# Another emission plan for a four-layer graph attention kernel: up to six weights per group, preparation begun in one-head steps, a tighter plan for late steps, another order of the last steps

## Chip, core and metric

The kernel runs on one core of one Trainium2 chip. The metric is device time in microseconds (us) of one execution; the median of several runs is given.

The engines are called by the names of the profile: PE is TensorE, DVE is VectorE, ACT is ScalarE, POOL is GpSimd, SP is SyncE, which here only issues transfers. Each engine works through its own instructions in the order in which the program issued them; engines wait for each other by semaphores.

## What is computed

Sixteen inputs x[b] of 1024 nodes with 256 features pass through four graph attention layers that share one adjacency matrix. All is fp32. Layers 0 and 2 have four heads of 64 features, layers 1 and 3 one head of 256. In short:

```python
for l in range(4):                                   # heads H = 4, 1, 4, 1
    h = relu(layernorm(x))                           # over the 256 features
    q = h @ W[l]                                     # split into H heads
    e = leaky_relu(q @ a_src [rows] + q @ a_dst [columns])
    attn = softmax(where(adj, e, -inf), over columns)
    x = x + elu(attn @ q)                            # layer 3: relu in place of elu
```

Layers 0 and 1 mask with adj > 0, layers 2 and 3 with adj != 0.

## The kernel before

**Steps.** A step is one layer of one input, so there are 16 x 4 = 64 steps, numbered 0 to 63 in the order of `order_of_steps`. Four inputs are in flight at a time (four streams); a stream's next layer can be prepared only when its last step has been added into x. The order takes turns over the streams, so that four-head steps and one-head steps mostly alternate. Steps 0, 1, 2 have four heads; in places two four-head steps meet (13 and 14, 21 and 22, 29 and 30, ...). The last ten steps before the change have 4, 1, 4, 1, 1, 4, 1, 4, 1, 1 heads.

**Weights.** The exponential of a leaky sum is written as a maximum of two products. With a row factor `g` (one value per target node, the same on all partitions), a column factor `rcol` (one value per source node) and the mask, a weight tile of 128 source nodes by 1024 target nodes is one DVE instruction:

```python
nc.vector.scalar_tensor_tensor(w, g, rcol[:, jc, h:h+1], mask[:, jc, :], op0=ALU.max, op1=ALU.mult)   # L250
```

A head has eight such tiles, so a four-head step has 32 and a one-head step 8. They lie in a ring of `WBUFS` = 19 buffers. `g` is in PSUM (two buffers): it is written to DRAM as `grow` (L227), fetched back to all partitions as `gs` (L239, two buffers) and copied to PSUM by ACT (L245, `broadcast`).

**Aggregation.** Every step has eight groups (`aggregate`). In a four-head step a group is one half of the target nodes of one head: four blocks of 128 nodes, each over eight weight tiles. In a one-head step it is one block of 128 nodes over all eight tiles. The matmuls (L266) write `acc` (two PSUM buffers), and ACT evicts it into `y` (L270). The ratio of `y` to its last column is the attention output. Below, "32 AGG2.4" means step 32, head 2, the group that starts at block 4.

**Preparation of a step** (`preparation`), in 18 pieces: statistics of x (DVE L161 `bn_stats`, L162 `bn_aggr`, then four POOL instructions, L165 to L169, that give `rstd` and `shift`), `normalise` in two halves (ACT L175, four instructions each, into a tile of a ring of three that `finish` shares), transposes (PE L183, with relu into `hT` by ACT L184), projections of eight blocks (PE L195, evicted into `whx` and `sd` by ACT L197 to L204, multiplied by POOL L206), `factors` (rcol, gcol) and `rows` (transposed gcol, written to `grow`).

**End of a step** (`finish`), in seven pieces that are issued during the next step: the reciprocal (DVE L287), the scaling of y and the negative part (POOL L291, L296), its exponential (ACT L300), and the sum into x (DVE L306 and POOL L307; in layer 3 DVE L309 and the store of the result by SP, L310, and the load of the stream's next input).

**The order of the work** is written out by a planner. Before every group it takes care that the weights of the group's head have been issued; after it, it issues what is due in `finish`, then what is due in the preparation of later steps (`prepare`, from a sorted `agenda`), and then some weights ahead: four in a four-head step, two in a one-head step, as far as buffers are free by program order (`done["free"] + WBUFS`). The due times are counted in groups: piece k of step n + 2 is due `PREPARATION[k]` groups after the begin of step n, or after its middle where the stream's last step is step n - 1 or n. A head's `g` can be issued once the whole preparation of its step has been. `fetch_heads` issues the `gs` transfers up to two heads ahead of `g`; it is called after `rows` and after every `g`.

## Time and profile before

| | us |
|---|---|
| median of 3 runs | 2754.75 (2754.04 to 2758.51) |
| profiled execution | 2758.29 |
| its span | 2756.5 |
| PE busy, weight loads busy | 2581.3, 2268.5 |
| DVE, ACT, POOL busy | 1984.5, 1199.6, 896.6 |
| weights (L250, DVE, 1280 tiles), busy | 1543.3 |
| `bn_stats`, `bn_aggr` (DVE, 512 each), busy | 200.7, 92.8 |
| aggregation matmuls, projections, transposes (PE), busy | 1965.4, 515.8, 155.4 |

A busy time is the time in which at least one instruction of the group ran. An engine's idle time is put down to the engine whose work released it last. Idle time of an engine costs nothing while another one sets the pace, so a view of the whole says less than one of a stretch: the first 95 us prepare the masks and the weights of the layers, the rest are the 64 steps of about 40 us each.

### The profile page before, as it was taken

The page shows a single profiled execution, that of the slowest core. Times are in us where ns is not written, and L with a number is a line of the kernel's source. Part 1 is how long each engine was busy: PE and PEld are TensorE (multiplying, and loading weights), DVE is VectorE, ACT ScalarE, POOL GpSimd, SP SyncE. Part 2 cuts the span into 40 slices and gives each one's busy share as a digit, 9 for nine tenths or more (in the row PEclk, how much of TensorE's full clock was granted, in tenths as well). Part 3 has the DMA queues.
Part 4 walks back from the last instruction along what each step waited for, and adds up shares of the span by engine and source line. Part 5 has one row for each costly group of instructions (what it writes and reads, how often), then busy time and mean ns, then how long its engine had stood idle before and what let it go on. Part 6 is the DMA issues. An engine that isn't in the chain of part 4 may idle for free.

```text
span 2756.5 us, 88771 instructions
## 1 busy us (share of the span) xinstructions
PE 2581.3 (94%) x40080; PEld 2268.5 (82%) x40080; DVE 1984.5 (72%) x2569; ACT 1199.6 (44%) x3265; POOL 896.6 (33%) x909
## 2 busy tenths in 40 slices
PE   1789988999999999999999999999999999999997
PEld 1688777888888888888888888888888888888876
DVE  5596855767966779747977679767797488775772
ACT  0534444444444444544444445444444444444341
POOL 0223333343332343342242343333323333433221
PEclk9999999999999999999999999999999999999998
DMA  4111010012211210111211111002112111101101
GB/s 138 62 49 40 10 40 25 25 36 67 72 36 44 71 49 25 41 39 47 88 41 48 62 40 41 33 17 71 56 49 71 34 46 64 34 17 39 56 25 39
DMA packets 63674, 130.08 MB, mean 47 GB/s; under 512 B 6208, under 2 KB 41792, under 8 KB 63296
## 3 DMA queue, kind: packets, MB, share of 16 engines
q1 hardware_dynamic: 60608, 123.35, 13.4%
q8 instruction: 315, 5.16, 0.8%
q10 hardware_dynamic: 2688, 1.05, 0.2%
q14 instruction: 63, 0.52, 0.1%
HBM read 106.95 MB, written 17.43 MB: 45 GB/s over the span
## 4 chain that ended last, share of the span: by engine, by line
PE 72%; DVE 14%; DMA 6%; ACT 4%; issue 3%; POOL 1%; DVEq 0%; ACTq 0%; SPq 0%; POOLq 0%
PE acc L266 53%; PE pp L195 15%; DVE w L250 11%; DMA gs<-grow 4%; PE pp L183 3%; DMA grow<-gT 2%; DVE bn L161 1%; ACT t L300 1%; ACT g L245 1%; DVE t L306 1%; DVE mv L162 1%; ACT whx L197 1%; DMA a_bc<-in_L_gnn_a 1%; ACT whx L201 0%; ACT y L270 0%
## 5 line engine op out<-in xcount | busy, mean ns | idle before, releaser
L266 PE MATMUL acc<-whx,w 128*64 128x65 f32 x36864 | 1965.4, 242 | 77.9 <-DVE w L250 56.9
L266 PEld LDWEIGHTS acc<-whx,w 128*64 128x64 f32 x36864 | 1764.3, 145 | 265.5 <-DVE w L250 78.7
L250 DVE SCALAR_TENSOR_TENSOR w<-g,rcol,mask 128x1024 f32<-128x1024 f32 x1280 | 1543.3, 1273 | 523.4 <-ACT g L245 432.7
L270 ACT ACTIVATE y<-acc 128x260 f32<-128x260 f32 (+1 forms) x512 | 196.8, 384 | 1071.1 <-PE acc L266 1069.8
L195 PE MATMUL pp<-wx,hT 128*128 128x258 f32 (+1 forms) x2048 | 515.8, 395 | 2.9 <-ACT hT L184 2.7
L291 POOL TENSOR_TENSOR y<-y,r 128x1024 f32<-128x1024 f32 x128 | 243.0, 1899 | 716.1 <-DVE r L287 716.1
L195 PEld LDWEIGHTS pp<-wx,hT 128*128 128x128 f32 x2048 | 378.3, 192 | 78.1 <-ACT hT L184 15.7
L307 POOL TENSOR_TENSOR x<-x,t 128x1024 f32<-128x1024 f32 x96 | 226.8, 2362 | 408.2 <-DVE t L306 399.6
L206 POOL TENSOR_TENSOR whx<-whx 128x256 f32<-128x256 f32 x256 | 157.5, 618 | 471.2 <-ACT whx L204 471.2
L175 ACT ACTIVATE t<-x,shift,rstd 128x256 f32<-128x256 f32 x512 | 264.8, 588 | 78.7 <-POOL x L307 56.6
L245 ACT ACTIVATE g<-gs 128x1024 f32<-128x1024 f32 x160 | 163.5, 1022 | 129.5 <-DMA gs<-grow 128.0
L197 ACT ACTIVATE whx<-pp,nbias 128x4 f32<-128x4 f32 (+1 forms) x512 | 135.5, 265 | 181.3 <-PE pp L195 169.7
L161 DVE BATCH_NORM_STATS2 bn<-x 128x6 f32<-128x256 f32 x512 | 200.7, 392 | 2.4 <-DMA x<-in_x 2.4
L183 PE MATMUL pp<-ident,t 128*128 128x128 f32 x1024 | 155.4, 284 | 34.0 <-ACT t L175 18.9
L183 PEld LDWEIGHTS pp<-ident,t 128*128 128x128 f32 x1024 | 111.3, 141 | 78.8 <-ACT whx L201 28.0
L184 ACT ACTIVATE hT<-pp 128x512 f32<-128x512 f32 x256 | 145.5, 593 | 19.2 <-PE pp L183 18.8
L306 DVE SCALAR_TENSOR_TENSOR t<-t,y 128x1024 f32<-128x1024 f32 x96 | 118.4, 1233 | 35.4 <-ACT t L300 35.3
L287 DVE RECIPROCAL r<-y 128x32 f32<-128x32 f32 (+1 forms) x64 | 17.6, 276 | 160.0 <-ACT y L270 159.9
L201 ACT ACTIVATE whx<-pp,whx 128x256 f32<-128x256 f32 x256 | 121.7, 475 | 0.0
L166 POOL TENSOR_TENSOR rstd<-rstd,neghalf 128x8 f32<-128x8 f32 x64 | 106.7, 1668 | 5.3
L162 DVE BATCH_NORM_AGGREGATE mv<-bn 128x2 f32<-128x6 f32 x512 | 92.8, 181 | 16.9
L296 POOL TENSOR_SCALAR t<-y 128x1024 f32<-128x1024 f32 x96 | 101.7, 1060 | 8.5
(37 smaller groups left out, 533.0 us busy)
## 6 DMA issues: line engine op xcount, KB each, us to landing
gs<-grow SPq DMA_DIRECT2D x160, 512.0 KB
x<-in_x SPq DMA_DIRECT2D x16, 1024.0 KB
out<-x SPq DMA_DIRECT2D x32, 512.0 KB
a_raw<-in_adj SPq DMA_DIRECT2D x8, 512.0 KB
a_bc<-in_L_gnn_a ACTq DMA_DIRECT2D x8, 128.0 KB
wx<-in_L_gnn_W SPq DMA_DIRECT2D x4, 256.0 KB
grow<-gT SPq DMA_DIRECT2D x32, 16.0 KB
grow<-gT SPq DMA_DIRECT2D x32, 4.0 KB
```

The source lines that it names most:

```text
L161: nc.vector.bn_stats(st["bn"][:, c, :], xs[b][:, c, :])
L175: nc.scalar.activation(xn[:, q, :], xs[b][:, c, :], AF.Identity, bias=st["shift"][:, c:c + 1], scale=st["rstd"][:, c:c + 1])
L183: nc.tensor.transpose(pt[:, q, :], st["xn", half][:, q, k * P:(k + 1) * P], ident)
L195: nc.tensor.matmul(pw, lhsT=st["hT", half][:, k, q * P:(q + 1) * P], rhs=wx[l][:, k, :], start=(k == 0), stop=(k == K - 1))
L197: nc.scalar.activation(whx[:, c, :, D], pw[:, F + H:F + 2 * H], AF.Exp, bias=nbias[l], scale=slope)
L206: nc.gpsimd.tensor_tensor(whx[:, c, :, 0:D], whx[:, c, :, 0:D], whx[:, c, :, D:D + 1].to_broadcast([P, H, D]), op=ALU.mult)
L245: nc.scalar.activation(g, state[n]["gs", h], AF.Copy)
L250: nc.vector.scalar_tensor_tensor(w, state[n]["g", h], state[n]["rcol"][:, jc, h:h + 1], masks[LAYERS[steps[n][1]][3]][:, jc, :], op0=ALU.m ...
L266: nc.tensor.matmul(acc[o % P:o % P + cols, q, :], lhsT=st["w", h, jc][:, o:o + cols], rhs=st["whx"][:, jc, h, :], start=(jc == 0), stop=(j ...
L270: nc.scalar.activation(st["y"][:, i0:i0 + per, h, :], acc, AF.Copy)
L291: nc.gpsimd.tensor_tensor(yh, yh, r[:, :, None].to_broadcast([P, HALF * H, D]), op=ALU.mult)
L307: nc.gpsimd.tensor_add(xh, xh, e)
```

## The change

- `bn_aggr` goes: mean and variance of the two halves that `bn_stats` gives are combined by POOL, in ten instructions of 8 columns in place of four.
- `normalise` gets a ring of two tiles for itself, `finish` another one of two, in place of a common ring of three; `WBUFS` becomes 18.
- Every step gets a time of begin: 8 (n - 2) groups, three groups earlier if step n - 3 has one head, later if the stream's last step demands it (five groups after that step's end, eight for a new input). Preparation is planned from it, by `PREPARATION`, or by the tighter `LATE` where the begin was put off. By this, steps 3, 5, 6, 8, 54, 56 and 63 are late ones.
- The `gs` transfers of a step may start right after `rows`; its first `g` comes two groups later, when the preparation is declared done by an empty last piece.
- Up to six weights ahead per group in four-head steps, three in one-head steps.
- The store of a result and the next load become pieces of their own, due in group 4.
- The last ten steps have another order of streams; the numbers of heads in them are 1, 4, 1, 4, 4, 1, 4, 1, 1, 1.

The diff:

```diff
--- before.py
+++ after.py
@@ -36,8 +36,10 @@
 SHIFT = 60.0
 EXP_SHIFT = math.exp(SHIFT)
 STREAMS = 4
-WBUFS = 19
-PREPARATION = (0, 0, 1, 2, 3, 3, 4, 4, 5, 5, 5, 5, 6, 6, 7, 7, 8, 9)
+WBUFS = 18
+
+PREPARATION = (0, 0, 2, 3, 4, 4, 5, 5, 6, 6, 6, 6, 7, 7, 8, 8, 9, 10, 10, 12)
+LATE = (0, 0, 1, 1, 2, 2, 3, 3, 3, 3, 3, 3, 4, 4, 4, 4, 5, 6, 6, 8)
 
 
 LAYERS = [
@@ -155,21 +157,29 @@
 
         def stats(half):
             if half == 0:
-                st["mv"] = small.tile([P, C, 2], F32, name="mv")
                 st["bn"] = small.tile([P, C, 6], F32, name="bn")
+            bn = st["bn"]
             for c in range(half * HALF, (half + 1) * HALF):
-                nc.vector.bn_stats(st["bn"][:, c, :], xs[b][:, c, :])
-                nc.vector.bn_aggr(st["mv"][:, c, :], st["bn"][:, c, :])
+                nc.vector.bn_stats(bn[:, c, :], xs[b][:, c, :])
             if half == 1:
+
+                m0, s0, m1, s1 = (bn[:, :, i] for i in (1, 2, 4, 5))
                 rstd = st["rstd"] = small.tile([P, C], F32, name="rstd")
-                nc.gpsimd.tensor_scalar(rstd, st["mv"][:, :, 1], EPS, None, op0=ALU.add)
+                shift = st["shift"] = small.tile([P, C], F32, name="shift")
+                dev = small.tile([P, C], F32, name="dev")
+                nc.gpsimd.tensor_tensor(dev, m0, m1, op=ALU.subtract)
+                nc.gpsimd.tensor_tensor(dev, dev, dev, op=ALU.mult)
+                nc.gpsimd.tensor_scalar(dev, dev, 0.25, EPS, op0=ALU.mult, op1=ALU.add)
+                nc.gpsimd.tensor_tensor(rstd, s0, s1, op=ALU.add)
+                nc.gpsimd.tensor_scalar(rstd, rstd, 1.0 / F, None, op0=ALU.mult)
+                nc.gpsimd.tensor_tensor(rstd, rstd, dev, op=ALU.add)
                 nc.gpsimd.tensor_tensor(rstd, rstd, neghalf, op=ALU.pow)
-                shift = st["shift"] = small.tile([P, C], F32, name="shift")
-                nc.gpsimd.tensor_tensor(shift, st["mv"][:, :, 0], rstd, op=ALU.mult)
-                nc.gpsimd.tensor_scalar(shift, shift, -1.0, None, op0=ALU.mult)
+                nc.gpsimd.tensor_tensor(shift, m0, m1, op=ALU.add)
+                nc.gpsimd.tensor_tensor(shift, shift, rstd, op=ALU.mult)
+                nc.gpsimd.tensor_scalar(shift, shift, -0.5, None, op0=ALU.mult)
 
         def normalise(half):
-            xn = st["xn", half] = prep.tile([P, HALF, F], F32, name="t4", bufs=3)
+            xn = st["xn", half] = prep.tile([P, HALF, F], F32, name="xn")
             for q in range(HALF):
                 c = half * HALF + q
                 nc.scalar.activation(xn[:, q, :], xs[b][:, c, :], AF.Identity,
@@ -231,7 +241,10 @@
             out += [lambda half=half, k=k: transpose(half, k) for k in range(K)]
             out += [lambda c=c: project(c) for c in range(half * HALF, (half + 1) * HALF)]
 
-        return list(zip(PREPARATION, out + [factors, rows], strict=True))
+
+        out += [factors, rows, lambda: fetch_heads(n + 1), lambda: None]
+        at = LATE if begin[n] > 8 * (n - 2) else PREPARATION
+        return [(begin[n] + k, piece) for k, piece in zip(at, out, strict=True)]
 
     def fetch(n, h):
 
@@ -292,7 +305,7 @@
                                     op=ALU.mult)
             if l < L - 1:
 
-                e = st["e", half] = prep.tile([P, HALF * H, D], F32, name="t4", bufs=3)
+                e = st["e", half] = prep.tile([P, HALF * H, D], F32, name="e")
                 nc.gpsimd.tensor_scalar(e, yh, 0.0, -3.0e38, op0=ALU.min, op1=ALU.max)
 
         def exponential(half):
@@ -307,6 +320,8 @@
                 nc.gpsimd.tensor_add(xh, xh, e)
                 return
             nc.vector.scalar_tensor_tensor(xh, yh, 0.0, xh, op0=ALU.max, op1=ALU.add)
+
+        def store(half):
             nc.sync.dma_start(
                 out=out[b, half * HALF * P:(half + 1) * HALF * P, :].rearrange(
                     "(c p) f -> p c f", p=P), in_=xs[b][:, half * HALF:(half + 1) * HALF, :])
@@ -315,7 +330,8 @@
 
         return [(0, divide), (0, lambda: scaled(0)), (1, lambda: scaled(1)),
                 (1, lambda: exponential(0)), (2, lambda: exponential(1)),
-                (2, lambda: add(0)), (3, lambda: add(1))]
+                (2, lambda: add(0)), (3, lambda: add(1))] + (
+                    [(4, lambda: store(0)), (4, lambda: store(1))] if l == L - 1 else [])
 
 
 
@@ -328,28 +344,28 @@
     tiles = [(n, h, jc) for n, (b, l) in enumerate(steps) for h in range(LAYERS[l][0])
              for jc in range(C)]
     place = {t: i for i, t in enumerate(tiles)}
-    done = {"tiles": 0, "g": 0, "gs": 0, "free": 0, "prepared": 0, "wanted": 0}
+    done = {"tiles": 0, "g": 0, "gs": 0, "rows": 0, "free": 0, "prepared": 0}
     agenda = []
 
     def prepare(upto):
 
-        while agenda and (agenda[0][0] <= upto or agenda[0][1] < done["wanted"]):
+        while agenda and agenda[0][0] <= upto:
             _, n, piece, last = agenda.pop(0)
             piece()
             if last:
                 done["prepared"] = n + 1
-                fetch_heads()
-
-    def plan(n, at):
+
+    def plan(n):
         new = preparation(n)
-        agenda.extend((at + k, n, piece, i == len(new) - 1) for i, (k, piece) in enumerate(new))
+        agenda.extend((at, n, piece, i == len(new) - 1) for i, (at, piece) in enumerate(new))
         agenda.sort(key=lambda a: a[:2])
 
-    def fetch_heads():
-
+    def fetch_heads(below=0):
+
+        done["rows"] = max(done["rows"], below)
         while done["gs"] < min(done["g"] + 2 * C, len(tiles)):
             n, h, _ = tiles[done["gs"]]
-            if n >= done["prepared"]:
+            if n >= done["rows"]:
                 break
             fetch(n, h)
             done["gs"] += C
@@ -363,8 +379,7 @@
                 if n >= done["prepared"]:
                     if i < done["g"] or not must:
                         break
-                    done["wanted"] = n + 1
-                    prepare(-1)
+                    prepare(max(a[0] for a in agenda if a[1] == n))
                 broadcast(n, h)
                 done["g"] += C
                 fetch_heads()
@@ -375,21 +390,27 @@
 
     for b in range(STREAMS):
         load(b)
-    ready_at = [-1] * len(steps)
-    last = {}
+    last, begin = {}, []
     for n, (b, l) in enumerate(steps):
-        ready_at[n] = last.get(b % STREAMS, -9)
+
+        early = n > 2 and LAYERS[steps[n - 3][1]][0] == 1
+        begin.append(8 * (n - 2) - (3 if early else 0) if n > 1 else -99)
+        if b % STREAMS in last:
+
+            begin[n] = max(begin[n], 8 * (last[b % STREAMS] + 1) + (8 if l == 0 else 5))
+        if n > 2:
+            begin[n] = max(begin[n], begin[n - 1] + (5 if begin[n] > 8 * (n - 2) else 3))
         last[b % STREAMS] = n
-    for n in range(2):
-        plan(n, -99)
-        prepare(0)
     ending = []
     with tc.manual_schedule():
+        for planned in (1, 2):
+            plan(planned - 1)
+            prepare(-1)
         for n in range(len(steps)):
             for k, (h, i0, per) in enumerate(groups(n)):
-
-                if n + 2 < len(steps) and k == (0 if ready_at[n + 2] < n - 1 else 4):
-                    plan(n + 2, 8 * n + k)
+                while planned < len(steps) and begin[planned] <= 8 * n + k:
+                    plan(planned)
+                    planned += 1
                 emit_tiles(place[n, h, C - 1] + 1, must=True)
                 aggregate(n, h, i0, per)
                 if i0 + per == C:
@@ -397,7 +418,7 @@
                 while ending and ending[0][0] <= k:
                     ending.pop(0)[1]()
                 prepare(8 * n + k)
-                ahead = 4 if per > 1 else 2
+                ahead = 6 if per > 1 else 3
                 emit_tiles(min(done["tiles"] + ahead, done["free"] + WBUFS))
             for _, piece in ending:
                 piece()
@@ -408,16 +429,11 @@
 
 def order_of_steps(B, L):
 
+
     depth = B // STREAMS * L
     one = [[(k // L * STREAMS + s, k % L) for k in range(depth)] for s in range(STREAMS)]
-    at = [0] * STREAMS
-    turns = [0, 1, 2, 0, 3, 2] + [0, 1, 2, 3] * depth
-    steps = []
-    for s in turns:
-        if at[s] < depth:
-            steps.append(one[s][at[s]])
-            at[s] += 1
-    return steps
+    turns = [0, 1, 2, 0, 3, 2] + [0, 1, 2, 3] * (depth - 4) + [1, 0, 3, 2, 1, 0, 3, 2, 1, 3]
+    return [one[s].pop(0) for s in turns]
 
 
 _OUT = ((16, 1024, 256), "float32")
```

## The prediction

> **What bounds the kernel now.** I read the page first (busy shares and slices), then the busy time by windows, then the matrix engine's own waits in three stretches, then VectorE's timeline around one pair of steps.
>
> ```profile
> PE 2581.3 (94%) x40080; PEld 2268.5 (82%) x40080; DVE 1984.5 (72%) x2569; ACT 1199.6 (44%) x3265; POOL 896.6 (33%) x909
> ...
> PE   1789988999999999999999999999999999999997
> ...
> DVE  5596855767966779747977679767797488775772
> ...
> PEclk9999999999999999999999999999999999999998
> ```
>
> PE is busy 94% of the span, so a change of order can win back only its idle 175 us. The dips are in the first ten slices and the last one.
>
> ```profile
> 0.00:95.00 95.00, 31.59 (x152) 24.28 (x153) 42.84 (x105) 19.27 (x59) 14.34 (x32) 0.98 0.38 120
> 95.00:300.00 205.00, 181.81 (x3652) 161.71 (x3651) 172.54 (x199) 80.84 (x211) 61.57 (x64) 0.96 0.13 42
> 300.00:530.00 230.00, 207.47 (x3322) 180.01 (x3322) 150.82 (x193) 98.55 (x268) 72.32 (x67) 0.96 0.09 27
> ```
>
> Window length, then PE busy first. The start to 95 us (63 us idle) is not touched. From 95 to 530 PE idles 23.2 + 22.5 = 45.7 us at a clock of 0.96. PE's waits by releaser (us, times, longest), for 95 to 530, then 530 to 2330, then 2330 to the end:
>
> ```profile
> PE acc L266 <- DVE w L250: 35.8, 49, 0.9
> PE pp L183 <- ACT t L175: 3.1, 4, 2.7
> ```
> ```profile
> PE acc L266 <- DVE w L250: 13.1, 20, 0.9
> PE acc L266 <- ACT y L270: 12.1, 14, 1.2
> ```
> ```profile
> PE acc L266 <- DVE w L250: 7.9, 15, 1.2
> PE acc L266 <- ACT y L270: 4.4, 4, 1.6
> ```
>
> So early PE waits for weights. In the middle it loses 36 us in 1800, a third of it to ScalarE, which stands in front of an eviction while it waits for a fetch. VectorE has room on average; it is late in places:
>
> ```profile
> 354.57 1.23 DVE L306 SCALAR_TENSOR_TENSOR t<-t,y 128x1024 f32<-128x1024 f32 x1 [4.62 <-ACT t L300]
> 378.10 9.63 DVE L250 SCALAR_TENSOR_TENSOR w<-g,rcol,mask 128x1024 f32<-128x1024 f32 x8 [22.30 <-ACT g L245]
> ```
>
> Here it idles 22.3 us in a one-head step and then falls behind in the four-head step after it.
>
> **The Trainium skill.** "TensorE: Matmul & The Clock Gate" (specification table at its head) gives ScalarE, VectorE and GpSimd a strict first-in-first-out queue; the trace agrees: ScalarE idled 128.0 us in front of `g` copies for the `gs` transfer. The same page, Part 1, says idleness lowers PE's clock; the 0.96 of the early windows against 1.00 later agrees. "SBUF — State Buffer" (SBUF: two separate sides) says a VectorE instruction with two SBUF inputs locks out a GpSimd one that reads SBUF. `w` has one tensor input in PSUM, so the new small GpSimd operations should not slow it; only L306 could meet them. No run here shows that.
>
> **The change, part by part.** Prices: `w` 1543.3/1280 = 1.206 us; `bn_stats` 0.392; a pair with `bn_aggr` 4.25 us for eight; L306 1.23; PE group of a four-head step 3.8 us, of a one-head step 3.6 (rows of the timeline); preparation on PE 10.1 us (four double projections of 1.94, two transpose pairs of 1.03, one of 0.27); `t` (L175) 2.1 us per half; `g` 1.0.
>
> *Statistics.* 512 `bn_aggr` go. VectorE gets 4.25 - 8 x 0.392 = 1.1 us per preparation, 70 us in all, worth something only where VectorE is late. GpSimd gets ten operations for four: six at 0.205, three at 0.25, `pow` 1.67, that is 3.65 against 2.37 us, and with gaps 0.09 a piece 4.5 against 2.7. The chain to `shift` is 1.8 us longer at the GpSimd end and 1.1 shorter at the VectorE end: at the start +1 us. Later, `normalise` stands two groups (about 10 us) after `stats`, which hides it. In a late step (LATE: one group) it does not: there ScalarE stands at L175, and PE's transposes behind it wait some 3.5 us, as the 2.7 above already shows. Behind a standing L175 on ScalarE are the eviction of the last group and the next `g`; PE has two `acc` slots, so it notices after one group. The ten operations read strided columns of `bn`, which no row shows; at 0.2 to 0.3 us each (the 128x8 rows) the chain is 4 to 5 us. GpSimd rises from 33% to 36%; its other work has 67% idle time as cover.
>
> *Steps 0 to 2* (four heads each). VectorE needs 96 x 1.206 = 116 us and PE 92 + 28 = 120 from 104 us on, so both must run without bubbles. Four weights per group let a bubble in at each `g` (1.4, 3.4, 1.8, 5.9 us before 251). With six, `g` of the next head is issued a group earlier. By queue order VectorE then runs through: from 97.6, 32 tiles and 3.1 us of statistics end at 139; step 1's at 180; step 2's at 228. PE ends step 2 near 237; the trace has 251. Gain 14.
>
> *Steps 3 to 8.* `rows` comes two groups before the first `g`, so ScalarE no longer stands for the transfer (grow and gs, 6 us). The first weights of step 6 come about 12.7 us before its group 0, against 4.8 now (378.1 to 382.9). Against that stand new waits: transposes of steps 5, 6, 8 behind late statistics, 3.5 + 1 + 3.4, and weights late by 2 to 3 us at the ends of steps 4 and 6. Summed by queue order, step 9 begins some 25 us earlier than now, 11 of them here. I take 22 for both, 10 to 32, since clock recovery is included.
>
> *Steps 9 to 53.* Fourteen four-head steps that follow a one-head step now get their first `g` after group 4 instead of group 1. VectorE, counted from the end of group 4: first `w` 3.3 (transposes 1.0, two hT 1.2, `g` 1.0), head 0 complete at 16.1 with statistics of 3.1 between; PE wants it after one transpose pair, three groups, three double projections and another pair (1.0 + 3 x 3.6 + 1.9 + 2.9 + 1.9 = 18.6). Between heads PE has two groups and two pieces of preparation, 7.6 + 3 to 4 us, VectorE eight tiles, 9.6, and every second head two L306. So head 1 is ready at 25.9 and wanted at 29.4; `g2` stands behind a `normalise`, ready 29.3, so head 2 at 38.9, wanted 42.2; head 3 at 51.0, wanted 53.7; the next step's eight tiles at 60.6, wanted 61.6. All hold, by 1 to 4 us. Where two four-head steps meet (21/22, 37/38) the second then waits about 7 us, by the same count that gives 2.9 for now; after an early begin (13/14, 29/30, 45/46) 2.3 against 6.2. Over both kinds nothing changes. What goes is the ScalarE wait: 12.1 to about 2. Gain 10 (0 to 18).
>
> *One buffer for weights less, own buffers for `xn` and `e`.* 18 still hold two heads and two tiles; the last tiles of a head wait a group longer where VectorE is far ahead anyway, costing nothing while the margins above hold. The split ends L175's waits for x<-x,t (56.6 us, 15 times); they lie beside PE work, and I count them within the 10.
>
> *Stores* are issued one or two groups later, so SP's queue with the `gs` fetches no longer stands behind them. The next x load follows 5 us later; its statistics come four groups (about 20 us) after, and its transfer took 6.1 us in the chain of waits. Zero; without that cover up to 5 us for each of 12 loads.
>
> *Last steps.* Now 18 us of waits from 2330 on. Step 63's owner finishes layer 2 as step 60 instead of 61, and three one-head steps end the run, so weights for 61 and 62 are early; step 63's last tile is late by about 1 instead of some 6. New: late statistics before 54 and 56, 3.5 each, and one four-head meeting, 57/58, 5. About 13 remain: gain 5, with the clock 6 (-4 to 12).
>
> Sum: 1 - 22 - 10 - 6 = -37. The profiled execution took 2758.3 (span 2756.5 and 1.8 around it), so 2721; the median of the runs is 3.5 lower, so **2718**.
>
> **Rivals.** *A, half of it:* the bubbles of steps 0 to 2 go, but elsewhere each removed fetch wait returns as a wait on `shift` or on the projections' PSUM slots. For it: L175 already waited 21.6 us for `shift`. Against it: only three waits. -14: 2741. *B, weights start too late:* the slack of 2.7 us in the four-head steps is my count of ScalarE's queue. If `g` comes one one-head group (5.0 us) later, each of the 20 steps so treated loses 2.3: 46, less the 37 gained, +9: 2764; two groups later, 7.3 each, 2860. It decides from about 4.6 us of delay. For it: VectorE's 22.3 us gap shows what a late `g` does, and one-head steps now start VectorE 7 us later than the trace. Against it: the fetch is done by then. *C, it doesn't do what it says:* where buffers bind, groups emit two tiles, not six, and only the statistics saving is left, hidden by PE: within 5 us. Against it: at heads' ends six fit.
>
> **How the numbers follow.** A measurement of this kernel can tell about 0.2%, 5.5 us. Forecast 0.53 (own range 2703 to 2735), A 0.22, C 0.08, B 0.17. The forecast and A are faster: 0.75; same 0.08; slower 0.17. The range runs from full early and middle gains, 2699, to B a little over its one-group case, 2768.
>
> **What would show it.** Right: PE waits on `w` before 530 fall from 35.8 to about 22; waits on y (L270 before) in the middle from 12.1 to 2; step 9 starts near 500 instead of 525; `t` waits on `shift` grow. Wrong: PE waits on `w` between 530 and 2330 well above 13.1, at the four-head steps after a one-head step (B); or `pp` waits on ACT `xn` above 20 us (A).

## Result: slower, and the profile after

The changed kernel takes 2781.65 us (median of 4 runs, 2777.85 to 2785.33), the kernel before on the same chip 2754.39. The ratio is 1.0098, with an interval of 1.0079 to 1.0117. Slower by 27 us, where 37 us of gain were forecast. The profiled execution of after took 2777.85 (span 2776.1), so it is 19.6 us longer than the profiled one before: the profile shows a little less of the loss than the medians do.

The page of after, busy shares and slices, as for before:

```profile
PE 2577.5 (93%) x40080; PEld 2274.2 (82%) x40080; DVE 1918.1 (69%) x2057; ACT 1211.5 (44%) x3265; POOL 985.7 (36%) x1293
...
PE   1699999999999998999999999999999999999998
...
PEclk9899999999999999999999999999999999999999
```

PE does the same work, VectorE 66 us less, GpSimd 89 us more. PE's dips to 8 in the third, sixth and seventh slices are gone, and a new one stands in the sixteenth; the clock is lower in the second slice, where the steps begin. So the change did what it says, and the loss is not spread evenly. To place it I read from the timeline the end of the first eviction of all (ACT L270 in before, L283 in after), of the first one of step 9, and of the last ones of steps 53 and 63 (us):

| stage | before | after | difference | forecast |
|---|---|---|---|---|
| start to the first eviction | 112.3 | 127.9 | +15.6 | +1 |
| to the first eviction of step 9 (called steps 0 to 8) | 424.2 | 387.3 | -36.9 | -22 |
| to the last eviction of step 53 (steps 9 to 53) | 1806.9 | 1852.0 | +45.1 | -10 |
| to the last eviction of step 63 | 402.4 | 398.1 | -4.3 | -6 |

Two stages gained, one of them more than forecast. Two lost, and each loss has its place in the trace.

**The start.** VectorE's first weights, before and then after (timeline, start and length in us, in brackets the idle time ahead and what ended it):

```profile
97.59 9.62 DVE L250 SCALAR_TENSOR_TENSOR w<-g,rcol,mask 128x1024 f32<-128x1024 f32 x8 [26.89 <-ACT g L245]
```
```profile
112.53 3.67 DVE L263 SCALAR_TENSOR_TENSOR w<-g,rcol,mask 128x1024 f32<-128x1024 f32 x3 [42.89 <-ACT g L258]
```

`g` comes 15 us later. In before, the preparations of steps 0 and 1 are issued ahead of `with tc.manual_schedule()`, and ScalarE's instructions do not stand in the order in which the program is written: the first copy of `g` comes ahead of the evictions of step 1's last projections (ScalarE's timeline):

```profile
96.50 1.05 ACT L245 ACTIVATE g<-gs 128x1024 f32<-128x1024 f32 x1
...
98.88 0.30 ACT L197 ACTIVATE whx<-pp,nbias 128x4 f32<-128x4 f32 x1
```

In after they are issued inside that block, where the written order holds. ScalarE has the preparation of step 0 done at 88.7 and then goes on with step 1:

```profile
88.72 0.27 ACT L235 ACTIVATE gT<-pp 32x128 f32<-32x128 f32 x1 [1.02 <-PE pp L233]
92.52 4.04 ACT L185 ACTIVATE xn<-x,shift,rstd 128x256 f32<-128x256 f32 x8 [3.54 <-POOL shift L179]
96.46 1.05 ACT L194 ACTIVATE hT<-pp 128x512 f32<-128x512 f32 x2
...
111.32 0.27 ACT L235 ACTIVATE gT<-pp 32x128 f32<-32x128 f32 x1 [1.02 <-PE pp L233]
111.49 1.95 ACT L258 ACTIVATE g<-gs 128x1024 f32<-128x1024 f32 x2
```

The first copies of `g` stand behind the whole of that, up to step 1's own `gT`.

**The middle.** PE's waits in after between 530 and 2330 us (us, times, longest), as for before:

```profile
PE acc L279 <- DVE w L263: 29.9, 39, 0.9
PE pp L233 <- POOL gcol L228: 22.2, 10, 3.0
PE pp L193 <- ACT whx L214: 5.2, 22, 0.2
PE pp L193 <- ACT whx L211: 4.7, 22, 0.2
PE pp L205 <- ACT gT L235: 3.7, 7, 0.6
PE pp L193 <- ACT xn L185: 2.7, 2, 2.6
```

The wait for ScalarE's `y`, 12.1 in before, is gone, as forecast. In its place PE stands 22.2 us for `gcol`, a line that before does not have in this stretch, and 16.8 us more for `w`. The `gcol` stops are seven of 2.95 us (in preparations during steps 15, 20, 23, 31, 36, 39, 47) and three of 0.5. GpSimd's timeline shows one of them, with PE's row below:

```profile
1422.47 0.21 POOL L170 TENSOR_TENSOR dev<-bn 128x8 f32<-128x8 f32 x1
...
1424.20 1.67 POOL L176 TENSOR_TENSOR rstd<-rstd,neghalf 128x8 f32<-128x8 f32 x1
...
1426.12 1.23 POOL L178 TENSOR_TENSOR shift<-shift,rstd 128x8 f32<-128x8 f32 x1
1427.44 0.24 POOL L179 TENSOR_SCALAR shift<-shift 128x8 f32<-128x8 f32 x1
1427.64 1.90 POOL L304 TENSOR_TENSOR y<-y,r 128x1024 f32<-128x1024 f32 x1
1429.63 1.04 POOL L309 TENSOR_SCALAR e<-y 128x1024 f32<-128x1024 f32 x1
1430.75 0.29 POOL L228 TENSOR_SCALAR gcol<-gcol 128x32 f32<-128x32 f32 x1
```
```profile
1431.09 0.40 PE L233 MATMUL pp<-ident,gcol 128*32 128x128 f32 x1 [2.95 <-POOL gcol L228]
```

From 1422.47 GpSimd runs with no gap over 0.1 us: the ten operations of another step's statistics, then the second half's scaling of `finish` (L304, L309), and only then the 0.29 us of `gcol`. ScalarE had delivered `gcol` at 1426.45. A GpSimd of which 36% is busy is late here because of what stands ahead in its queue. Over all preparations of the stage the trace shows the same: in the seven stops of 2.95 us the other step's statistics and the scaling both stand in one unbroken run ahead of `gcol`, in the three of 0.5 us the statistics alone, and everywhere else neither, and PE does not stop. By the plan the seven are the places where this step and the one after it both begin without the three groups' lead, so that the next step's statistics come one group ahead of this one's `factors`.

The clock adds to it. Busy time by windows around the same stop (window length, PE busy first; PEclk is the column ahead of the last two):

```profile
1427.00:1430.60 3.60, 1.14 (x6) 0.65 (x4) 0.29 (x1) 0.38 (x1) 3.42 (x4) 1.00 0.00 0
1430.60:1434.00 3.40, 2.91 (x8) 2.35 (x9) 2.21 (x1) 3.18 (x6) 2.68 (x3) 0.51 0.02 7
1434.00:1444.00 10.00, 10.00 (x52) 8.78 (x51) 2.16 (x3) 4.74 (x9) 2.36 (x1) 1.00 0.38 126
```

For 3.4 us after the stop PE has half its clock. "TensorE: Matmul & The Clock Gate" of the Trainium skill (Part 1) speaks of idle windows of some 3.4 us; this stop is 2.95. Four of the seven stops of 2.95 us brought a window of half clock. The same is found without any long stop, where PE runs at VectorE's pace at the end of a four-head step (PE's timeline, then windows):

```profile
725.66 0.34 PE L279 MATMUL acc<-whx,w 128*64 128x65 f32 x4 [0.55 <-DVE w L263]
726.85 0.34 PE L279 MATMUL acc<-whx,w 128*64 128x65 f32 x4 [0.86 <-DVE w L263]
728.05 0.48 PE L279 MATMUL acc<-whx,w 128*64 128x65 f32 x4 [0.85 <-DVE w L263]
729.24 2.00 PE L279 MATMUL acc<-whx,w 128*64 128x65 f32 x32 [0.71 <-DVE w L263]
```
```profile
717.00:727.50 10.50, 8.78 (x287) 8.37 (x282) 10.50 (x16) 2.79 (x5) 9.36 (x14) 1.00 0.01 3
727.50:734.30 6.80, 5.55 (x98) 5.36 (x100) 6.80 (x7) 6.06 (x11) 2.74 (x2) 0.50 0.01 2
```

Three or four waits of up to 0.86 us in a row, one for each weight tile, are enough.

The clock records of the traces say when. Within a trace the granted clock changes only at multiples of 3.41 us. I cut the time from the first to the last eviction of all fourteen traces (before, after and the twelve experiments) on that grid and took PE's idle time in every stretch that ran at full clock. After more than 2.0 us idle the next stretch ran at half clock, 103 times out of 103; after less than 1.2 us never; between the two, 85 times out of 211. So what counts is the idle time within one such stretch, not the length of a single stop. Of the four stops that brought half clock, 2.36 us or more lay in one stretch; the other three are cut by a border, with 1.96 us at most on one side.

Added up from the granted clock in the trace, PE has half its clock for 6.8 us of the stage of steps 9 to 53 in before and for 44.4 in after: 23.9 behind such rows of `w` waits, 13.7 behind `gcol` stops, 6.8 behind an `xn` wait.

The account of the middle has two parts. PE's idle time in the stage rises from 36.6 to 71.0 us, by 34.4; the waits explain 33.3 of it: `gcol` +22.2, `w` +16.8, `gT` +3.7, `xn` +2.7, `y` -12.1. PE's busy time rises from 1770.3 to 1781.0, by 10.7 us, for the same work; as far as the trace tells, that is what 37.6 us more at half clock cost here. Half of 37.6, 18.8, would be the upper bound: where PE waits for weights anyway, a slower clock is partly hidden. Together that is the 45.1 us measured, about three quarters of it waiting.

### The profile page after: what moved, and what is told of

Read it like the earlier page. It is cut to its first block, busy times and chain, and to the rows that moved or that the text cites. A ratio compares the mean times of both kernels' runs of the same rounds, so it can differ in the third digit from the quotient of the medians.

```text
span 2776.1 us, 89366 instructions
## 1 busy us (share of the span) xinstructions
PE 2577.5 (93%) x40080; PEld 2274.2 (82%) x40080; DVE 1918.1 (69%) x2057; ACT 1211.5 (44%) x3265; POOL 985.7 (36%) x1293
## 4 chain that ended last, share of the span: by engine, by line
PE 73%; DVE 13%; issue 5%; POOL 4%; ACT 4%; DMA 1%; DVEq 0%; ACTq 0%; SPq 0%; POOLq 0%
PE acc L279 53%; PE pp L205 16%; DVE w L263 10%; PE pp L193 3%; DVE bn L163 1%; POOL rstd L176 1%; ACT whx L207 1%; POOL y L304 1%; ACT xn L185 1%; ACT whx L211 1%; DMA a_bc<-in_L_gnn_a 1%; ACT whx L214 0%; POOL shift L178 0%; ACT e L313 0%; DVE e L319 0%
## 5 line engine op out<-in xcount | busy, mean ns | idle before, releaser
L283 ACT ACTIVATE y<-acc 128x260 f32<-128x260 f32 (+1 forms) x512 | 197.8, 386 | 1152.9 <-PE acc L279 1152.6
L304 POOL TENSOR_TENSOR y<-y,r 128x1024 f32<-128x1024 f32 x128 | 242.4, 1897 | 307.5 <-DVE r L300 302.9
L320 POOL TENSOR_TENSOR x<-x,e 128x1024 f32<-128x1024 f32 x96 | 227.2, 2367 | 239.3 <-DVE e L319 235.2
L319 DVE SCALAR_TENSOR_TENSOR e<-e,y 128x1024 f32<-128x1024 f32 x96 | 132.7, 1382 | 230.6 <-ACT e L313 230.6
L185 ACT ACTIVATE xn<-x,shift,rstd 128x256 f32<-128x256 f32 x512 | 263.5, 590 | 36.9 <-POOL shift L179 36.9
L193 PE MATMUL pp<-ident,xn 128*128 128x128 f32 x1024 | 160.6, 286 | 46.7 <-ACT xn L185 32.0
L193 PEld LDWEIGHTS pp<-ident,xn 128*128 128x128 f32 x1024 | 113.3, 142 | 94.3 <-ACT xn L185 40.4
L228 POOL TENSOR_SCALAR gcol<-gcol 128x32 f32<-128x32 f32 (+1 forms) x64 | 25.3, 396 | 460.8 <-ACT gcol L226 459.2
L163 DVE BATCH_NORM_STATS2 bn<-x 128x6 f32<-128x256 f32 x512 | 171.3, 407 | 3.9 <-DMA x<-in_x 2.7
L313 ACT ACTIVATE e<-e 128x1024 f32<-128x1024 f32 x96 | 100.9, 1051 | 62.2 <-POOL e L309 61.8
L300 DVE RECIPROCAL r<-y 128x32 f32<-128x32 f32 (+1 forms) x64 | 17.5, 273 | 131.4 <-ACT y L283 131.4
```

Source lines behind the costliest of these rows:

```text
L163: nc.vector.bn_stats(bn[:, c, :], xs[b][:, c, :])
L185: nc.scalar.activation(xn[:, q, :], xs[b][:, c, :], AF.Identity, bias=st["shift"][:, c:c + 1], scale=st["rstd"][:, c:c + 1])
L193: nc.tensor.transpose(pt[:, q, :], st["xn", half][:, q, k * P:(k + 1) * P], ident)
L283: nc.scalar.activation(st["y"][:, i0:i0 + per, h, :], acc, AF.Copy)
L304: nc.gpsimd.tensor_tensor(yh, yh, r[:, :, None].to_broadcast([P, HALF * H, D]), op=ALU.mult)
L320: nc.gpsimd.tensor_add(xh, xh, e)
```

## Experiments

Each kernel below is after or before with one edit, or a combination of edits. The batches ran on different chips, each with its own runs of before (medians 2755.05, 2756.53 and 2751.82), so between batches the ratios are the safer comparison. Where a recorded expectation uses letters for the theories: S is the start (preparation moved into the written order), G is `gcol` standing behind the scaling in GpSimd's queue, P is that the ten statistics operations on GpSimd are what is too long, V is that VectorE needs the time that `bn_aggr` took. The stages of each profiled execution, read as in the table above (us), and the time at half clock in the middle stage. Each row is one execution. x_both and x_order have the same plan for nearly all of the middle and differ there by 4.2 us and by 13.7 us of half clock, so smaller differences in these columns are not told apart:

| kernel | start | steps 0-8 | steps 9-53 | steps 54-63 | half clock, 9-53 |
|---|---|---|---|---|---|
| before | 112.3 | 424.2 | 1806.9 | 402.4 | 6.8 |
| after | 127.9 | 387.3 | 1852.0 | 398.1 | 44.4 |
| a_start | 111.4 | 390.3 | 1851.9 | 398.2 | 44.4 |
| a_factors | 129.8 | 387.6 | 1824.6 | 391.4 | 34.1 |
| a_aggr | 125.8 | 396.8 | 1853.8 | 400.5 | 54.6 |
| b_start | 126.4 | 424.3 | 1806.3 | 399.0 | 3.4 |
| b_gcol | 111.3 | 448.3 | 1832.0 | 412.8 | 0.0 |
| x_both | 112.4 | 386.9 | 1824.7 | 388.7 | 41.0 |
| x_ahead | 112.5 | 405.8 | 1861.5 | 405.4 | 47.8 |
| x_order | 111.5 | 387.1 | 1820.5 | 406.2 | 27.3 |
| x_ready | 112.2 | 393.6 | 1805.2 | 393.8 | 13.7 |
| x_aggr | 112.9 | 393.0 | 1842.7 | 393.9 | 58.0 |
| x_ring | 112.0 | 390.9 | 1823.6 | 392.1 | 41.0 |
| x_late | 113.5 | 382.6 | 1803.4 | 388.2 | 6.8 |

**a_start: only the start's order, out of after.**

```diff
+    for planned in (1, 2):
+        plan(planned - 1)
+        prepare(-1)
     with tc.manual_schedule():
-        for planned in (1, 2):
-            plan(planned - 1)
-            prepare(-1)
```

> The changed kernel, with the preparation of steps 0 and 1 issued ahead of the block whose instructions keep the written order, as in the kernel before. Theory S (the written order put the first g copies behind all of step 1's preparation): the first weight comes at about 97.5 us instead of 112.5, and the time falls by 13 to 17, to about 2766. Rival (the ten GpSimd operations of the statistics delay the start): the first weight stays near 112, no change in time.

2766.47 (2764.32 to 2772.01), ratio 1.0038 (1.0024 to 1.0052): 15 us less than after. VectorE's first weights are back where they were in before:

```profile
96.62 3.67 DVE L263 SCALAR_TENSOR_TENSOR w<-g,rcol,mask 128x1024 f32<-128x1024 f32 x3 [26.26 <-ACT g L258]
```

The start's column moves by 16.5 us; steps 0 to 8 take 3 us more, and the rest stays.

**b_start: the same move put into before.**

```diff
-    for n in range(2):
-        plan(n, -99)
-        prepare(0)
     ending = []
     with tc.manual_schedule():
+        for n in range(2):
+            plan(n, -99)
+            prepare(0)
```

> The kernel before, with the preparation of steps 0 and 1 issued within the block that keeps the written order, as in the changed kernel. Theory S: slower by 13 to 17, about 2769, first weight near 112 us. Rival: the start of the changed kernel is late because of its statistics, and this stays within 4 of 2754.

2770.12, against 2755.05 of before in the same batch, ratio 1.0053 (1.0036 to 1.0070): 15 us more; in the stages only the first column grows. The start is settled from both sides.

**a_factors: `factors` one group earlier, so that `gcol` is ahead of the second half's scaling (and, at the seven stops, of the other step's statistics too).**

```diff
-PREPARATION = (0, 0, 2, 3, 4, 4, 5, 5, 6, 6, 6, 6, 7, 7, 8, 8, 9, 10, 10, 12)
-LATE = (0, 0, 1, 1, 2, 2, 3, 3, 3, 3, 3, 3, 4, 4, 4, 4, 5, 6, 6, 8)
+PREPARATION = (0, 0, 2, 3, 4, 4, 5, 5, 6, 6, 6, 6, 7, 7, 8, 8, 8, 10, 10, 12)
+LATE = (0, 0, 1, 1, 2, 2, 3, 3, 3, 3, 3, 3, 4, 4, 4, 4, 4, 6, 6, 8)
```

> The changed kernel, with the piece factors due one group earlier, ahead of the scaling of the second half on GpSimd; rows stays. Theory G (gcol stands on GpSimd behind the two instructions for the second half of y, 2.94 us, and the matrix engine stands at the transpose of gcol, and each such stop brings a half-clock window): waits of the matrix engine on gcol fall from 34.7 to below 8 us, half-clock windows between 526 and 2330 us from about ten to five, time falls by 25 to 40. Theory W (weights begin too late in one-head steps, and that is the loss): waits on gcol fall, but the time by 10 at most, since the weights are then the next to be late.

2744.21, ratio 0.9954 (0.9937 to 0.9971): 37 us less than after, and faster than before. PE's waits for `gcol` in the whole of after, and then in a_factors, where the view of L233 gives them:

```profile
PE pp L233 <- POOL gcol L228: 34.7, 18, 3.0
```
```profile
  POOL gcol L228: 3.5, 2
```

31 us of stops went; what is left stands in the start. Half clock in the middle is 10 us less, which is within the scatter. The `w` waits stayed: 30.6 in the middle against 29.9. So the two are separate. The edit takes `gcol` out from behind the statistics and the scaling at once; it does not say which of the two matters more.

**a_aggr: after with the statistics of before (`bn_aggr` on VectorE, four GpSimd operations).**

```diff
             for c in range(half * HALF, (half + 1) * HALF):
-                nc.vector.bn_stats(bn[:, c, :], xs[b][:, c, :])
+                nc.vector.bn_stats(st["bn"][:, c, :], xs[b][:, c, :])
+                nc.vector.bn_aggr(st["mv"][:, c, :], st["bn"][:, c, :])
...
```

> The changed kernel, with the statistics of the kernel before (bn_aggr on VectorE, four GpSimd operations). Theory P (the longer GpSimd chain delays gcol and shift): waits on gcol fall from 34.7 to about 15 and those on xn from 32 to about 25, time falls by 10 to 25. Theory G (gcol's place behind the scaling decides): waits on gcol stay within 6 of 34.7, time within 6. Theory V (VectorE is short of time): 1.1 us more per preparation on VectorE makes it slower by 10 or more.

2788.1, ratio 1.0116 (1.0100 to 1.0132): 6 us slower than after by the medians, but the intervals of the ratios overlap. PE's waits in the middle:

```profile
PE acc L271 <- DVE w L255: 39.0, 48, 1.3
PE pp L225 <- POOL gcol L220: 10.4, 10, 1.2
```

Two effects that nearly cancel. Each of the seven long stops falls from 2.95 to 1.24 us, by 1.7: that is the longer chain on GpSimd, whose cost the prediction had as 1.8 us. But the `w` waits rise by 9 us (the half clock, by 10, is within the scatter). Neither P nor V alone is right; the statistics' move adds to the `gcol` stop and relieves VectorE at once. G is not right by itself either: with four operations instead of ten ahead of the scaling, less than half of the stop is left.

**b_gcol: `factors` and `rows` one group later, in before.**

```diff
-PREPARATION = (0, 0, 1, 2, 3, 3, 4, 4, 5, 5, 5, 5, 6, 6, 7, 7, 8, 9)
+PREPARATION = (0, 0, 1, 2, 3, 3, 4, 4, 5, 5, 5, 5, 6, 6, 7, 7, 9, 10)
```

> The kernel before, with factors and rows both one group later, so that factors comes behind the scaling of the second half of y on GpSimd, as in the changed kernel. Theory G: waits of the matrix engine on gcol rise from 3 to 15 to 30 us, and the time by 15 to 35. Rival (the four-instruction statistics leave GpSimd enough room, only the changed kernel's ten make gcol late): waits on gcol below 8, time within 8.

2821.54, ratio 1.0253 (1.0237 to 1.0268), 70 us slower: far more than expected. PE's waits in the middle:

```profile
PE acc L266 <- DVE w L250: 28.3, 38, 0.9
PE pp L223 <- POOL gcol L218: 10.7, 15, 0.7
PE pp L195 <- ACT hT L184: 9.5, 21, 1.1
```

The `gcol` stops appear, but at 0.7 us at most; with four operations for the statistics GpSimd is probably through earlier, which was not traced further. What weighs more is that `rows`, and with it every first `g`, is a group later: `w` waits 28.3 against 13.1 in the middle, and in steps 0 to 8, where nothing was spare, 24 us with 65 us at half clock against 34. The middle lost 25.1 us; `gcol` 10.7, `hT` 9.5, `w` +15.2 and `y` -12.1 make 23.3. The edit moves two things, so it does not measure the `gcol` stop by itself.

**x_both: after with the edits of a_start and a_factors together.**

> The changed kernel with both edits tried one by one: the start outside the block of written order, and factors one group earlier. If the two losses are separate (theory): they add, 2781.6 - 15 - 37 = 2729, that is 26 below the kernel before, near the forecast of 2718. Rival (they share the half-clock windows, or the gain of one is taken up by late weights): 2740 or more.

2726.63 (2725.19 to 2729.97), ratio 0.9893 (0.9879 to 0.9906). The two add up: 2781.65 less 15 and 37 gives 2729. With both mended the change gains. The middle is still 18 us longer than in before: PE idles 11.9 us more there, where `w` is the largest wait, and is busy 5.9 us longer, at half clock for 41.0 us against 6.8:

```profile
PE acc L279 <- DVE w L263: 30.4, 40, 0.9
```

**x_ahead: x_both with four and two weights ahead per group, as in before.**

```diff
-                ahead = 6 if per > 1 else 3
+                ahead = 4 if per > 1 else 2
```

> As x_both, with four weights ahead per group of a four-head step and two of a one-head step, as in the kernel before. Theory (six keep VectorE going in steps 0 to 2 and in the four-head steps): slower than x_both by 8 to 20, waits of the matrix engine on w up by 10 or more. Rival (the number is only an order of issue, and VectorE would run through either way): within 4 of x_both.

2799.8, ratio 1.0154 (1.0139 to 1.0168): 73 us slower than x_both, far more than the 8 to 20 expected, in all stages (19 in steps 0 to 8, 37 in the middle, 17 at the end). `w` waits of PE in the middle:

```profile
PE acc L279 <- DVE w L263: 53.7, 74, 0.9
```

Without six per group, the new plan with its later `g` is slower than before.

**x_ready: x_both with a step declared prepared one group after `rows` instead of two (late steps keep two).**

```diff
-PREPARATION = (0, 0, 2, 3, 4, 4, 5, 5, 6, 6, 6, 6, 7, 7, 8, 8, 8, 10, 10, 12)
+PREPARATION = (0, 0, 2, 3, 4, 4, 5, 5, 6, 6, 6, 6, 7, 7, 8, 8, 8, 10, 10, 11)
```

> As x_both, with the first g of a step one group after rows instead of two, so 5 us earlier in one-head steps. Theory W (the remaining waits on w, 30.6 us in the middle, come from weights that begin too late): waits on w in the middle fall to 20 or less, and the time by 8 to 15. Rival T (one group is too short for the transfer of gs, so ScalarE stands in front of evictions again as in the kernel before): waits on y return with 5 or more, time within 4 or slower.

2718.41 (2717.81 to 2720.22), ratio 0.9862 (0.9849 to 0.9876). In the middle:

```profile
PE acc L279 <- DVE w L263: 17.2, 23, 0.9
PE pp L193 <- ACT xn L185: 6.5, 1, 6.5
```

The first `g` a group earlier takes 13 us of `w` waits and 27 us of half clock out of the middle, which is now as long as in before. ScalarE's wait for the `gs` transfer comes back:

```profile
ACT g L258 <- DMA gs<-grow: 54.5, 24, 4.1
```

It costs PE little: no wait for `y` appears, but PE waits 4.1 us in the middle for `hT`, which ScalarE writes. What PE pays besides are longer waits for `xn` in the late steps' preparations, 5.5 to 6.5 us each during steps 3, 52 and 54, against 2.7 to 2.8 in x_both.

**x_late: x_ready with the late steps' statistics one group earlier, the rest of `LATE` at the same time as before.**

```diff
-LATE = (0, 0, 1, 1, 2, 2, 3, 3, 3, 3, 3, 3, 4, 4, 4, 4, 4, 6, 6, 8)
+LATE = (0, 0, 2, 2, 3, 3, 4, 4, 4, 4, 4, 4, 5, 5, 5, 5, 5, 7, 7, 9)
...
-            begin[n] = max(begin[n], 8 * (last[b % STREAMS] + 1) + (8 if l == 0 else 5))
+            begin[n] = max(begin[n], 8 * (last[b % STREAMS] + 1) + (8 if l == 0 else 4))
         if n > 2:
-            begin[n] = max(begin[n], begin[n - 1] + (5 if begin[n] > 8 * (n - 2) else 3))
+            begin[n] = max(begin[n], begin[n - 1] + (4 if begin[n] > 8 * (n - 2) else 3))
```

> As x_ready (2718), with the statistics of the late steps one group earlier (begin four groups after the stream's last step instead of five, all other pieces of LATE one later, so where they were). Theory L (in late steps the transposes wait for statistics that stand behind weights on VectorE): waits on xn fall from 38 to about 22, time by 8 to 16, to about 2706. Rival (the statistics then wait for the sum into x on GpSimd, and weights behind them are late): waits on w rise by as much, time within 4 of 2718.

2700.23 (2700.05 to 2700.77), ratio 0.9814 (0.9798 to 0.9830): the best version, 1.9% below before. Against x_ready it gains 13 us by the ratios, as expected (18 by the medians). The `xn` waits of the whole run fall from 38.0 to 24.0 us, the half clock over the span from 48.2 to 33.8 (69.0 in before), and PE is busy 95% of the span:

```profile
PE 2550.6 (95%) x40080; PEld 2254.1 (84%) x40080; DVE 1916.2 (71%) x2057; ACT 1207.4 (45%) x3265; POOL 976.0 (36%) x1293
```

**x_order: x_both with before's order of the last steps.**

```diff
-    turns = [0, 1, 2, 0, 3, 2] + [0, 1, 2, 3] * (depth - 4) + [1, 0, 3, 2, 1, 0, 3, 2, 1, 3]
-    return [one[s].pop(0) for s in turns]
+    turns = [0, 1, 2, 0, 3, 2] + [0, 1, 2, 3] * depth
...
```

> As x_both, with the last ten steps in the order of the kernel before. There the last two steps stand two apart in their stream, so by the new rule step 63's preparation begins in group 5 of step 62 and the rest of it is issued at once at its end. Theory (the new order is what lets the new rule work at the end): slower than x_both by 15 to 30. Rival (the new order by itself gains some 5): slower by 5 at most.

2740.39, ratio 0.9945 (0.9932 to 0.9959): 14 us slower than x_both, a little under the 15 to 30 expected, with 17.5 us more in the last ten steps.

**x_aggr: x_both with the statistics of before (the edit of a_aggr).**

> As x_both, with the statistics of the kernel before (bn_aggr on VectorE, four GpSimd operations). Theory V (VectorE is late in places, and the 1.1 us per preparation count there, now that gcol no longer hides it): slower than x_both by 8 to 20, waits on w up by 8 or more. Rival P (the shorter GpSimd chain pays as well): within 5 of x_both; waits on xn down by 3 to 8.

2752.22 (12 runs), ratio 1.0003 (0.9995 to 1.0012), against 0.9893 of x_both: 26 us by the medians, 30 by the ratios. V is right here, at more than its figure. `w` waits in the middle:

```profile
PE acc L271 <- DVE w L255: 39.4, 49, 1.3
```

9 us more than in x_both, and half clock in the middle 58.0 us against 41.0. With `gcol` out of the way, nothing offsets the loss of VectorE's time as it did in a_aggr.

**x_ring: x_both with a common ring of three for `xn` and `e`, and 19 weight buffers, as in before.**

```diff
-WBUFS = 18
+WBUFS = 19
...
-            xn = st["xn", half] = prep.tile([P, HALF, F], F32, name="xn")
+            xn = st["xn", half] = prep.tile([P, HALF, F], F32, name="t4", bufs=3)
...
-                e = st["e", half] = prep.tile([P, HALF * H, D], F32, name="e")
+                e = st["e", half] = prep.tile([P, HALF * H, D], F32, name="t4", bufs=3)
```

> As x_both, with the buffers of the kernel before: one ring of three for xn and e, 19 weight buffers. Theory (the ring of three makes normalise wait for the sum into x, as L175 waited 56.6 us before): slower than x_both by 5 to 20, with a wait of ScalarE's xn on GpSimd's sum into x of 40 us or more. Rival (the nineteenth weight buffer is worth as much): within 4.

2730.41 (2724.39 to 2731.33), ratio 0.9919 (0.9904 to 0.9934) against 0.9893 (0.9879 to 0.9906). The intervals overlap: the separate rings are worth 4 us by the medians and 7 by the ratios, and it may be nothing. The wait of ScalarE for GpSimd's sum into x that was expected is there, 42.0 us, but PE's waits for `w` in the middle, 28.8 us, are no longer than the 30.4 of x_both.

## Why the prediction was wrong, and where it was right

- **Failed: "at the start +1 us".** It measured +15.6. The step counted the statistics' chain alone. That the two first preparations move into the block with the written order stood in the diff and was not priced at all; to walk ScalarE's queue there, as the prediction did for a standing L175 in a late step, would have shown `g` behind step 1's preparation. a_start and b_start show it both ways, 15 us each.
- **Failed: *Steps 9 to 53*, "Gain 10 (0 to 18)".** It measured a loss of 45. Three terms were missing or mis-sized. *GpSimd's queue was not walked*: the prediction said "its other work has 67% idle time as cover", an average, where `factors` at +9 stands behind the statistics of one step and the scaling of another in one unbroken run of 8.3 us. That is 22.2 us of stops in the middle, 34.7 in all, and a_factors took 37 us away with it. *"Over both kinds nothing changes"* for the `w` waits: they rose by 16.8, mostly at the four-head steps 19, 35 and 51 (3.6 to 5.0 us each), where two one-head steps go ahead. VectorE's side of the count was right: in step 19, counted from the end of the eviction of group 4 of the step before, the first weight starts at 3.1 (3.3 in the count) and head 1 is complete at 24.9 (25.9). PE's side was not. It supposed one course of PE's work for all fourteen steps, in which head 1 is wanted at 29.4; that is near what the trace has in steps 16, 21 and 37, where PE is through with head 0 at 27.8 and does not wait for head 1. In steps 19, 35 and 51 it is through at 21.7, and stands. x_ready shows that one group of `g` is what lacked, since its 17.2 us are near the 13.1 of before. *The clock* in the middle was priced at nothing, and cost 10.7 us.
- **Right in mechanism: the wait for `gs`.** PE's wait for `y` fell from 12.1 us to nothing. But x_ready, where ScalarE waits for `gs` again and PE hardly notices (4.1 us for `hT`, none for `y`), shows that little of this was what the later `g` was needed for. In the mended kernel it cost more than it gave.
- **Right in mechanism, wrong in size: steps 0 to 8.** -36.9 against -22, outside its 10 to 32. `w` waits before 530 fell from 35.8 to 16.5, against "about 22", and time at half clock in this stage from 34.1 to 10.2. PE idles 20.0 us less in the stage and is busy 17.0 us less for the same work, so the clock's share was counted too small here too. x_ahead gives back 19 of it, so half is the six weights per group; what the rest owes to earlier begins and to VectorE's saved time was not separated; x_aggr gives back 6.
- **Near by chance: the last steps**, -4.3 against -6. The -4.3 includes 6.8 us of `gcol` stops that the forecast did not have; without those (x_both) it is -13.7, outside its -4 to 12. That the new order gains was right: x_order puts it, within the new plan, at 14 to 17 us.
- **Rivals.** B named the sign and a mechanism that is there, late weights, but at 2.3 us in each of 20 steps; it came at about 1 to 5 us in some of them, and it is the smaller part. A's sign, waits for `xn` above 20 us, did not come: 2.7 in the middle, 13.5 from 95 us on. C is out, x_ahead shows that six per group act. No rival had a queue on GpSimd. (B's two-group case comes to 2864 by its own sum, not 2860.)
- **The statistics** ("70 us in all, worth something only where VectorE is late") were worth 26 to 30 us in the mended kernel. VectorE, at 69% busy, is late in more places than I had allowed.

That x_ready comes to 2718.4, the number predicted, confirms the mechanism of no step: its early gain is larger than forecast, its middle gains 2 instead of 10.

One question stays open. No run took the half clock away and left the waits as they are, so its 10.7 us in the middle are read from PE's busy time in one trace of each kernel and not tried.

## To carry to other kernels

Price a moved piece on every engine that it touches, by walking that engine's queue at the new place: an engine that is 36% busy can still hold the pace-setter up with 0.3 us of work that stands behind 8 us of others' work. When pieces move into or out of a block whose order is kept as written, treat it as an edit of its own, and look at what now stands ahead of the first result. Count a row of short waits of the matrix engine as a clock loss too (here once they filled about half of a 3.41 us stretch), and look for the remedy at the producer's start (one group of `g`) rather than at its average load.

## What the runs showed of the hardware that was not expected

- Half clock needs no single long stop. Rows of three or four waits of up to 0.86 us, each after some 0.34 us of matmuls, brought 3.4 or 6.8 us at a granted clock of 0.5 in after, a_factors and x_both. In b_gcol, where the waits in the middle come singly or in pairs and are 1.1 us at most (for `w`, `gcol`, `hT`), there was none in that stage. The grid of 3.41 us above, with its 1.2 to 2.0 us of idle time, covers both, and the single stops too.
- L178, a GpSimd operation on 128x8 that reads SBUF, took 1.23 us instead of some 0.2, while VectorE's sum with two SBUF inputs ran beside it:

```profile
1426.06 1.23 DVE L319 SCALAR_TENSOR_TENSOR e<-e,y 128x1024 f32<-128x1024 f32 x1 [8.73 <-ACT e L313]
...
1426.12 1.23 POOL L178 TENSOR_TENSOR shift<-shift,rstd 128x8 f32<-128x8 f32 x1
```

  It goes the other way too. The next L319 took 2.65 us beside a GpSimd sum that had begun first:

```profile
1431.00 2.36 POOL L320 TENSOR_TENSOR x<-x,e 128x1024 f32<-128x1024 f32 x1
...
1431.79 2.65 DVE L319 SCALAR_TENSOR_TENSOR e<-e,y 128x1024 f32<-128x1024 f32 x1 [4.50 <-ACT e L313]
```

  The traces have many of both. In after nine of the 64 L178 fall beside such a sum of VectorE, and they take 1.22 to 1.23 us; the other 55 take at most 0.21. In a_factors, where the order on GpSimd is another, no L178 meets a sum and none takes over 0.21; there it is L177 that does, and that takes up to 1.13. In before the operation L168 on 128x8 never meets one and takes at most 0.21. L319's median is 1.224 us. In after it began 35 times while a GpSimd instruction was running, and each time it ended 1.08 to 1.09 us after that one's end, whether 0.14 or 1.58 us of that one were left when it began, as if its work had stood until then. This agrees with what "SBUF — State Buffer" (SBUF: two separate sides) says of a lock that the first comer holds for its whole instruction; the prediction had said that no run showed it. In the stop shown above it lengthened the chain ahead of `gcol` by 1 us.
